# Layer 0's own part turned on VectorE and loaded from DRAM, two-direction operand products, fixed operand slots

## The chip, the cores and the metric

The kernel runs on one core of a Trainium2 chip. A core has a matrix engine (TensorE; PE in the profile, PEld for its weight loads), VectorE (DVE), ScalarE (ACT), GpSimd (POOL) and SyncE (SP), which here only issues DMAs. Sixteen DMA engines move data between DRAM and the on-chip memory SBUF. Matmul results go to PSUM, which has eight banks. Each engine works through its own instruction queue in order and waits on semaphores for the others.

The metric is the device time of one execution in microseconds. The time of the kernel before is a median of 2452.59 us over 3 runs (2452.18 to 2453.55).

## The reference

Two graph layers over 128 graphs of 64 nodes with 768 features, all in float32. The change touches only layer 0:

```python
h = jnp.maximum(_layernorm(x, axis=-1), 0.0)
ctx = jnp.matmul(adj, hs @ Wadj.T + badj) / deg_c[..., None]
ctx = ctx + jnp.matmul(radj, hs @ Wrev.T + brev) / rdeg_c[..., None]
ctx = ctx + hs @ Wself.T + bself
...
x = x + ctx + rel
```

Here `hs` is `h`, `adj` is the 0/1 (and id) matrix of a graph, `radj` its transpose, and `rel` a relation term that is computed through small tables of counts. So every node's new value has three parts that go through a 768x768 weight matrix: its neighbours along the edges, its neighbours against them, and itself. Layer 1 is graph attention with six heads, an exponential linear unit and a sigmoid gate. It is left as it is.

## The kernel before

Two graphs make a tile of 128 rows; the 64 tiles are worked in 32 pairs. For a tile, layer 0 needs the transposes of (adjacency / degree) x h for the two directions, and the transpose of h for the self part, as stationary operands of matmuls. `operands` (L582) makes them on TensorE: it multiplies a block of h (64 rows of one graph, 128 features) by `rts`, which holds for each graph two scaled adjacency matrices and an identity, side by side, 192 columns. So one product gives all three parts, turned, in PSUM, and a ScalarE copy (L599) brings 768 columns of them to SBUF. One call makes the operand `a{k}{q}` of tile k of the pair and a third q of the features; there are six calls per pair.

`main` (L609) multiplies the operands by the weights. It doesn't take all 18 block products but 15: `form` (L602) makes sums of operands (A_SUMS: f1 to f11) on VectorE, sums of weight blocks are made once, and 15 products of six matmuls each (L638) go to four PSUM banks, a to d. When a bank holds a partial sum that belongs to the output, VectorE adds it into x (`add`, L630 and L632), and the bank is then used further. Ninety such matmul steps make a pair's main loop. Pair 0 uses the plain 18 products.

`beside` (L780) lists what is done beside the main loop of pair p, each entry with the step before which it is emitted: for pair p-1 the end (`finish`: layer norm of the result for layer 1, output store, stores of two forms of it), for pair p+1 the preparation (adjacency, degrees, layer norm and relu, operands, sums of operands, counts). `merged` (L233) sorts the entries by step, entries of one step in the order of the list. All five queues, SP's too, are then executed in exactly this order: nothing is reordered in layer 0.

The order around the change, in the loop of pair p, is: step 0 the sums f5, f6, f3 of pair p; 20 degrees and relus of pair p+1; 30 `prep_c`; 32 layer-norm statistics of the first finished tile; 37 and 43 counts; 40 `norm_and_store` of it (VectorE's scaled mean L292, ScalarE's relu L671, GpSimd's addition L672, then SP's output store L673 and the store L676 of hh); 44 `turn_and_store` (VectorE's 32x32 block transpose L682 and SP's store L683); 46 two calls of `operands`; 49 statistics of the second tile; 53 sum f1; 55 and 59 its `norm_and_store` and `turn_and_store`; 58 two calls; 66 sums f7, f4 and the loads of pair p+2's adjacency and x; 70 two calls; 77 sums f8, f9, f2. Operands lie in a rotating set of 17 buffers named `op` and two named `oq`.

```python
(46, lambda: operands(n, 1, 2)),
(46, lambda: operands(n, 1, 1)),
(53, lambda: form(n, "f1")),
...
(58, lambda: operands(n, 0, 0)),
(58, lambda: operands(n, 0, 2)),
...
(70, lambda: operands(n, 1, 0)),
(70, lambda: operands(n, 0, 1)),
```

For layer 1 the kernel already has a way to turn a tile without TensorE: `turn_and_store` transposes 32x32 blocks on VectorE and stores them to DRAM, and `load_h` (L326) loads them back in pieces of 32 floats, which puts the blocks in their places. `load_h(0)` is emitted at step 30 of the last pair's loop, among the loads of layer 1's weights (`fetch`, L337).

## Time and profile before

| What | us |
|---|---|
| median of 3 runs | 2452.59 |
| the profiled execution's own time | 2452.42 |
| its span, first to last instruction | 2450.6 |
| TensorE busy | 2424.8 (99%) |
| VectorE busy | 2047.8 (84%) |
| ScalarE busy | 1025.6 (42%) |
| the main products of layer 0 in bank a (L638 pwa) | 547.7 |
| the products that make operands (L591) | 152.0 |
| the copies of operands (L599) | 121.1 |

The span is the time between the first and the last instruction of the profiled execution. Busy time is the union of an engine's instructions; a matmul record's end is modelled, and records overlap. A float32 matmul is two records. In the lists of instructions a line gives the code line, the engine, the operation, output and inputs by name, shapes, the count, and after the bar busy time, mean length of one in ns and the idle time of the engine before them with what ended most of it. In lines of waits the numbers are total us, times and the longest one.

### The profile page before, as it was taken

What the parts mean: (1) busy time and instruction counts of PE and PEld (TensorE: products, weight loads), DVE (VectorE), ACT (ScalarE), POOL (GpSimd) and SP (SyncE); (2) the same over time, 40 slices, a digit from 0 to 9 for tenths busy, and PEclk for the clock granted to TensorE, in tenths of its full rate; (3) what the DMA queues carried; (4) which work ended last, traced back from release to release, by engine and by line L of the source; (5) the groups of instructions that cost most, each with busy time, mean ns of one, the idle gap of its engine ahead of it and who ended that gap; (6) DMA issues with size and microseconds to landing.
All of it is one profiled execution on the core that took longest, in us unless ns stands there. A gap on an engine that the chain in (4) does not pass through costs nothing.

```text
span 2450.6 us, 34880 instructions
## 1 busy us (share of the span) xinstructions
PE 2424.8 (99%) x11777; PEld 1689.8 (69%) x11777; DVE 2047.8 (84%) x4169; ACT 1025.6 (42%) x3399; POOL 449.2 (18%) x799
## 2 busy tenths in 40 slices
PE   9999999999999999999999998999999999999997
PEld 7888888888888888888888885444444444444445
DVE  8888788788788788788788767789999989888999
ACT  2122222222222222122122122776777777777677
POOL 1112112112112112112122112111111111111122
PEclk9999999999999999999999999999999999999999
DMA  5112212212213113113113146565555555555544
GB/s 181 55 54 90 73 54 92 70 55 95 67 54 99 64 54 102 60 54 108 55 55 108 54 115 161 91 119 116 113 109 113 113 108 115 108 107 118 109 98 101
DMA packets 348660, 224.54 MB, mean 92 GB/s; under 512 B 236234, under 2 KB 298813, under 8 KB 348482
## 3 DMA queue, kind: packets, MB, share of 16 engines
q1 hardware_dynamic: 338610, 197.51, 30.0%
q0 software_dynamic: 9728, 24.78, 6.4%
q8 instruction: 92, 1.51, 0.2%
q14 instruction: 86, 0.70, 0.1%
q10 hardware_dynamic: 144, 0.04, 0.0%
HBM read 96.07 MB, written 100.66 MB: 80 GB/s over the span
## 4 chain that ended last, share of the span: by engine, by line
PE 93%; DVE 4%; ACT 1%; DMA 1%; issue 0%; SPq 0%; DVEq 0%; POOL 0%; ACTq 0%; POOLq 0%
PE pwa L638 20%; PE pwb L638 16%; PE pma L908 13%; PE pmb L908 11%; PE pwc L638 7%; PE pwd L638 7%; PE pb L591 6%; PE pmc L908 4%; PE pmd L908 4%; PE ps L1061 2%; PE pwd L622 1%; PE ps L1043 1%; DVE weights L309 1%; ACT pr L960 1%; PE ps L1012 0%
## 5 line engine op out<-in xcount | busy, mean ns | idle before, releaser
L638 PE MATMUL pwa<-weights,op 128*128 128x256 f32 x2304 | 547.7, 382 | 4.1 <-DVE x L630 2.6
L638 PEld LDWEIGHTS pwa<-weights,op 128*128 128x128 f32 x2304 | 420.8, 190 | 66.9 <-issue 7.6
L638 PE MATMUL pwb<-weights,op 128*128 128x256 f32 x1536 | 360.8, 381 | 0.3 <-DVE x L630 0.3
L638 PEld LDWEIGHTS pwb<-weights,op 128*128 128x128 f32 x1536 | 286.6, 190 | 44.4 <-issue 6.7
L908 PE MATMUL pma<-weights,op_f 128*128 128x512 f32 x620 | 310.3, 597 | 1.1 <-DVE weights L935 0.8
L288 POOL TENSOR_TENSOR rn<-ve,mhalf 128x1 f32<-128x1 f32 x128 | 93.5, 730 | 935.4 <-DVE ve L287 935.3
L309 DVE TENSOR_TENSOR op<-op 128x768 f32<-128x768 f32 x248 | 241.4, 993 | 1.2
L960 ACT ACTIVATE pr<-pr 128x128 f32<-128x128 f32 x768 | 225.3, 295 | 25.1 <-DVE pr L950 24.1
L488 ACT ACTIVATE h<-x,rn 128x768 f32<-128x768 f32 x64 | 62.4, 1020 | 383.1 <-DVE rn L292 364.2
L671 ACT ACTIVATE hf<-x,rn 128x768 f32<-128x768 f32 x64 | 65.7, 1027 | 357.6 <-DVE rn L292 349.3
L908 PEld LDWEIGHTS pma<-weights,op_f 128*128 128x128 f32 x620 | 112.2, 190 | 138.7 <-issue 103.2
L599 ACT COPY op<-pb 128x768 f32<-128x768 f32 x160 | 121.1, 797 | 180.0 <-PE pb L591 179.8
L908 PE MATMUL pmb<-weights,op_f 128*128 128x512 f32 x372 | 193.1, 601 | 0.4 <-DVE hz L935 0.4
L638 PE MATMUL pwc<-weights,op 128*128 128x256 f32 x780 | 187.0, 383 | 0.0
L638 PE MATMUL pwd<-weights,op 128*128 128x256 f32 x768 | 176.3, 379 | 0.0
L638 PEld LDWEIGHTS pwc<-weights,op 128*128 128x128 f32 x780 | 145.6, 190 | 25.2 <-issue 6.7
L672 POOL TENSOR_TENSOR x<-x,hf 128x768 f32<-128x768 f32 x64 | 135.7, 2121 | 133.4 <-ACT hf L671 133.4
L638 PEld LDWEIGHTS pwd<-weights,op 128*128 128x128 f32 x768 | 145.8, 190 | 20.0 <-issue 0.2
L591 PE MATMUL pb<-r,h 64*128 64x192 f32 x1536 | 152.0, 337 | 0.4 <-ACT h L488 0.4
L591 PEld LDWEIGHTS pb<-r,h 64*128 64x128 f32 x1536 | 123.0, 187 | 33.9 <-issue 23.0
L960 ACT ACTIVATION_READ_ACCUMULATOR pr<-pr 128x1 f32 x768 | 144.3, 188 | 0.0
L1033 ACT ACTIVATE pb<-al,mx 128x64 f32<-128x64 f32 x384 | 128.5, 337 | 12.4 <-DVE mx L1025 11.6
(210 smaller groups left out, 4143.6 us busy)
## 6 DMA issues: line engine op xcount, KB each, us to landing
x<-in_x_dram SPq DMA_DIRECT2D x64, 384.0 KB
out_dram<-x SPq DMA_DIRECT2D x64, 384.0 KB
hh<-hh SPq DMA_DIRECT2D x64, 384.0 KB
h<-ht SPq DMA_DIRECT2D x64, 384.0 KB
h<-h SPq DMA_DIRECT2D x256, 96.0 KB
x<-hh SPq DMA_DIRECT2D x64, 384.0 KB
out_dram<-f POOLq DMA_DIRECT2D x62, 384.0 KB, 4.7
hx<-weights SPq DMA_DIRECT2D x88, 192.0 KB
```

What stands on the lines that cost most here:

```text
L288: nc.gpsimd.tensor_tensor(to[:, 0:1], ve, mhalf, op=OP.pow)
L309: return (nc.vector.tensor_add if s1 == "+" else nc.vector.tensor_sub)(to, x, y)
L488: nc.scalar.activation(h, X[t], AF.Relu, scale=to[:, 0:1], bias=to[:, 1:2])
L591: nc.tensor.matmul(ps[:, g, i * 3 * N : (i + 1) * 3 * N], H0[t][s, kb * P : (kb + 1) * P], rts[p % 2][s, k].rearrange("p s n -> p (s n)"), ...
L599: nc.scalar.copy(a.rearrange("p h s (g n) -> p g (h s) n", g=GT), ps[:, :, : 6 * N].rearrange("p g (x n) -> p g x n", n=N))
L638: nc.tensor.matmul(bank[b][:, :CQ], OPS[p, an][:, q, s, :], bw[bn][:, (s * KQ + q) * CQ : (s * KQ + q + 1) * CQ], start=(first and q == s ...
L671: nc.scalar.activation(h, X[t], AF.Relu, scale=to[:, 0:1], bias=to[:, 1:2])
L672: nc.gpsimd.tensor_add(X[t], X[t], h)
L908: nc.tensor.matmul(bank[p, b], operand(p, an)[:, q, :], bw2[bn][:, 2 * q * CQ : 2 * (q + 1) * CQ], start=(first and q == 0), stop=(q == KQ ...
L960: nc.scalar.activation(PR[t][:, j, h, :], PR[t][:, j, h, :], AF.Copy, accum_out=to)
L1033: nc.scalar.activation(PB[t][:, h, :], AL[t][:, h, :], AF.Exp, bias=MX[t][:, h : h + 1], accum_out=DN[t][:, h : h + 1])
L1061: nc.tensor.matmul(po[r][o, c, :], PT[t][s, c, o], (hs if r == g else HX[t])[s, 2 * c + r, :], start=True, stop=True)
```

## The change

The self part no longer goes through TensorE for pairs 2 to 31. ScalarE computes the relu of a tile a second time (`relu_mixed`) with the columns of each 128-feature block permuted. VectorE transposes the 32x32 blocks of that (`turn_own`, steps 27 and 33), SP stores the result to a DRAM tile (H0D), and `load_own` (steps 40, 44 and 60, two operands at a time) loads it as the third part of the operand's buffer, in pieces of 32 floats. `operands` now takes two calls in one PSUM tile and multiplies by two directions only, 128 columns; the calls are one batch at step 70 and two at step 46, none at 58. The buffers of operands become named slots (`SLOTS`), each with its own tag, two of them double, and f3 and f2 are formed in place of a12 and a10. The order of the dimensions in an operand changes (part before half). Pairs 0 and 1 keep the products of three directions. `load_h(0)` moves from step 30 to step 62 of the last pair's loop.

```diff
 PLAIN = tuple((f"a{k}{j}", f"b{j}{q}", "abcdab"[2 * i + k], j == 0, f"{k}{q}" if j == 2 else None,
                "+", i > 0) for i, q in enumerate((0, 2, 1)) for k in range(2) for j in range(3))
+SLOTS = {"a12": "s0", "f3": "s0", "a00": "s1", "a02": "s2", "a01": "s3", "f1": "s4", "f7": "s5",
+         "f11": "s5", "f4": "s6", "f8": "s7", "f9": "s8", "f5": "s9", "f6": "s10", "f10": "s11",
+         "a11": "t0", "a10": "t1", "f2": "t1"}
+SLOTS0 = {"a00": "s7", "a01": "s9", "a02": "s10", "a12": "s11"}
+IN_PLACE = {"f3": "a12", "f2": "a10"}
 PLACES = ("g6", "g10", "b11", "b21", "g12", "w", "g14", "b01", "b10", "b20", "b02", "b12", "b22",
...
     NQ = P // Q
+    H0D = [dram.tile([KB * P, P], F32, name=f"h0_{t}") for t in range(NT)]
     H1D = [[dram.tile([KB * P, P], F32, name=f"h1_{p}_{k}") for k in range(2)] for p in range(NP)]
     def row(v, parts):
...
                     to[:, :, s, :],
                     src.rearrange("(j k p) n -> j p k n", k=KQ, p=P)[j][:, :, q * CQ : (q + 1) * CQ])
-        return ([(30, lambda: load_h(0)), (67, lambda: nc.sync.dma_start(hbb, row(hb, P)))]
+        return ([(62, lambda: load_h(0)), (67, lambda: nc.sync.dma_start(hbb, row(hb, P)))]
                 + [(i, lambda n=n: load_block(n)) for i, n in (
                     (7, "b10"), (13, "b00"), (13, "b21"), (25, "b11"), (31, "b01"), (37, "b20"),
                     (49, "b22"), (49, "b02"), (61, "b12"))]
...
             h = H0[t] = work.tile([P, D], F32, name="h0")
             nc.scalar.activation(h, X[t], AF.Relu, scale=to[:, 0:1], bias=to[:, 1:2])
+        HP = {}
+        def relu_mixed(t, to):
+            hp = HP[t] = work.tile([P, D], F32, name="hp", bufs=1)
+            nc.scalar.activation(
+                hp.rearrange("p (b f i) -> p b f i", b=KB, f=NQ),
+                X[t].rearrange("p (b i f) -> p b f i", b=KB, f=NQ),
+                AF.Relu, scale=to[:, 0:1], bias=to[:, 1:2])
+        def turn_own(t):
+            h = work.tile([P, D], F32, name="hpt", bufs=1)
+            nc.vector.transpose(h, HP[t])
+            nc.sync.dma_start(H0D[t].rearrange("(b p) n -> p b n", p=P),
+                              h.rearrange("p (b n) -> p b n", b=KB))
+        def new_operand(p, n):
+            tag = SLOTS0.get(n, SLOTS[n]) if p == 0 else SLOTS[n]
+            OPS[p, n] = work.tile([P, 3, KQ, P], F32, name="op", tag=tag,
+                                  bufs=2 if tag[0] == "t" else 1)
+            return OPS[p, n]
+        def load_own(p, *names):
+            for n in names:
+                k, q = int(n[1]), int(n[2])
+                nc.sync.dma_start(
+                    new_operand(p, n)[:, 2].rearrange("p b (a n) -> p (b a) n", a=NQ),
+                    H0D[2 * p + k].rearrange("(b i) (f n) -> (i f) b n", i=Q, n=Q)[
+                        :, q * KQ * NQ : (q + 1) * KQ * NQ, :])
         def prep(p):
             af = ADF[p] = work.tile([P, 2, 2, N], F32, name="af", bufs=1)
...
             for i, (a, b) in enumerate(PARTS):
                 nc.scalar.copy(cn[: 3 * (b - a), i, :], pn[: 3 * (b - a), i, :])
-        def operands(p, k, q):
-            t = 2 * p + k
+        def operands(p, *calls):
+            n = 2 if p in SHARED else 3
             ps = pss.tile([P, GT, 512], F32, name="pb")
-            for i in range(2):
-                kb = 2 * q + i
-                for g in range(GT):
-                    s = slice(g * N, (g + 1) * N)
-                    nc.tensor.matmul(ps[:, g, i * 3 * N : (i + 1) * 3 * N],
-                                     H0[t][s, kb * P : (kb + 1) * P],
-                                     rts[p % 2][s, k].rearrange("p s n -> p (s n)"),
-                                     start=True, stop=True)
-            a = OPS[p, f"a{k}{q}"] = (
-                work.tile([P, KQ, 3, P], F32, name="oq") if (k, q) == (1, 1) else
-                work.tile([P, KQ, 3, P], F32, name="op", bufs=17))
-            nc.scalar.copy(a.rearrange("p h s (g n) -> p g (h s) n", g=GT),
-                           ps[:, :, : 6 * N].rearrange("p g (x n) -> p g x n", n=N))
+            for c, (k, q) in enumerate(calls):
+                to = ps[:, :, c * n * KQ * N : (c + 1) * n * KQ * N].rearrange(
+                    "p g (s i n) -> p g s i n", s=n, i=KQ)
+                for i in range(KQ):
+                    kb = KQ * q + i
+                    for g in range(GT):
+                        o = slice(g * N, (g + 1) * N)
+                        nc.tensor.matmul(to[:, g, :, i, :],
+                                         H0[2 * p + k][o, kb * P : (kb + 1) * P],
+                                         rts[p % 2][o, k, :n].rearrange("p s n -> p (s n)"),
+                                         start=True, stop=True)
+            for c, (k, q) in enumerate(calls):
+                a = OPS[p, f"a{k}{q}"] if p in SHARED else new_operand(p, f"a{k}{q}")
+                nc.scalar.copy(
+                    a[:, :n].rearrange("p s h (g n) -> p g (s h) n", g=GT),
+                    ps[:, :, c * n * KQ * N : (c + 1) * n * KQ * N].rearrange(
+                        "p g (x n) -> p g x n", n=N))
+        SHARED = range(2, NP)
         def form(p, *names):
             for n in names:
                 s0, x, s1, y = A_SUMS[n]
-                t = OPS[p, n] = work.tile([P, KQ, 3, P], F32, name="op", bufs=17)
-                signed(t, s0, OPS[p, x], s1, OPS[p, y])
+                if n in IN_PLACE:
+                    OPS[p, n] = OPS[p, IN_PLACE[n]]
+                else:
+                    new_operand(p, n)
+                signed(OPS[p, n], s0, OPS[p, x], s1, OPS[p, y])
         def main(p):
...
                     if first and q == s == 0:
                         new(b)
                     nc.tensor.matmul(
-                        bank[b][:, :CQ], OPS[p, an][:, q, s, :],
+                        bank[b][:, :CQ], OPS[p, an][:, s, q, :],
                         bw[bn][:, (s * KQ + q) * CQ : (s * KQ + q + 1) * CQ],
                         start=(first and q == s == 0), stop=(q == KQ - 1 and s == 2),
                         skip_group_check=True)
...
             DEV[p] = deviations((2 * p, 2 * p + 1))
         def relus(p):
+            to, mv = DEV[p]
             for k in range(2):
-                mean_and_relu(2 * p + k, DEV[p][0][k], DEV[p][1][k])
+                t = 2 * p + k
+                if p in SHARED:
+                    scaled_mean(to[k], mv[k])
+                    relu_mixed(t, to[k])
+                    relu(t, to[k])
+                else:
+                    mean_and_relu(t, to[k], mv[k])
         def degrees_and_norms(p):
             rd = degrees(p)
...
-            (54, lambda: operands(1, 1, 2)),
-            (54, lambda: operands(1, 1, 1)),
+            (54, lambda: operands(1, (1, 2))),
+            (54, lambda: operands(1, (1, 1))),
...
                 (30, lambda: prep_c(n)),
                 (37, lambda: ids_worth(n, 0)),
                 (43, lambda: ids_sum(n, 0)),
-                (46, lambda: operands(n, 1, 2)),
-                (46, lambda: operands(n, 1, 1)),
+                (27, lambda: turn_own(2 * n)),
+                (33, lambda: turn_own(2 * n + 1)),
+                (40, lambda: load_own(n, "a12", "a11")),
+                (44, lambda: load_own(n, "a00", "a02")),
+                (60, lambda: load_own(n, "a10", "a01")),
+                (46, lambda: operands(n, (1, 2), (1, 1))),
+                (46, lambda: operands(n, (0, 0), (0, 2))),
                 (53, lambda: form(n, "f1")),
                 (56, lambda: ids_worth(n, 1)),
-                (58, lambda: operands(n, 0, 0)),
-                (58, lambda: operands(n, 0, 2)),
                 (61, lambda: ids_sum(n, 1)),
                 (64, lambda: digits(n)),
                 (66, lambda: form(n, "f7", "f4")),
                 (66, lambda: load(n + 1)),
-                (70, lambda: operands(n, 1, 0)),
-                (70, lambda: operands(n, 0, 1)),
+                (70, lambda: operands(n, (1, 0), (0, 1))),
                 (77, lambda: form(n, "f8", "f9", "f2")),
                 (80, lambda: count_t(n, 0)),
                 (85, lambda: count_t(n, 1))]
```

More of the change, by code (lines that the diff above doesn't have):

```diff
@@ L718 @@
         table_product(0)
-        operands(0, 0, 0)
+        operands(0, (0, 0))
         table_product(1)
@@ L722 @@
         table_copy()
-        operands(0, 0, 1)
+        operands(0, (0, 1))
         prep_c(0)
@@ L748 @@
             (2, lambda: ids_sum(0, 0)),
-            (4, lambda: operands(0, 0, 2)),
+            (4, lambda: operands(0, (0, 2))),
             (8, lambda: count(0, 1)),
-            (12, lambda: operands(0, 1, 0)),
-            (12, lambda: operands(0, 1, 1)),
-            (17, lambda: operands(0, 1, 2)),
+            (12, lambda: operands(0, (1, 0))),
+            (12, lambda: operands(0, (1, 1))),
+            (17, lambda: operands(0, (1, 2))),
             (18, lambda: table_part(0)),
@@ L774 @@
             (60, lambda: weights_sums("g12", "g5")),
-            (64, lambda: operands(1, 0, 0)),
-            (64, lambda: operands(1, 0, 2)),
+            (64, lambda: operands(1, (0, 0))),
+            (64, lambda: operands(1, (0, 2))),
             (66, lambda: weights_sums("g8")),
@@ L779 @@
             (76, lambda: weights_sums("g11", "g3")),
-            (80, lambda: operands(1, 1, 0)),
-            (80, lambda: operands(1, 0, 1)),
+            (80, lambda: operands(1, (1, 0))),
+            (80, lambda: operands(1, (0, 1))),
             (84, lambda: count_t(1, 0)),
```

## The prediction, made before the result was known

> **What bounds the kernel now.** I read the page first: the busy shares, the forty slices, the costly groups.

> ```profile
> span 2450.6 us, 34880 instructions
> ...
> PE 2424.8 (99%) x11777; PEld 1689.8 (69%) x11777; DVE 2047.8 (84%) x4169; ACT 1025.6 (42%) x3399; POOL 449.2 (18%) x799
> ...
> L591 PE MATMUL pb<-r,h 64*128 64x192 f32 x1536 | 152.0, 337 | 0.4 <-ACT h L488 0.4
> L591 PEld LDWEIGHTS pb<-r,h 64*128 64x128 f32 x1536 | 123.0, 187 | 33.9 <-issue 23.0
> L599 ACT COPY op<-pb 128x768 f32<-128x768 f32 x160 | 121.1, 797 | 180.0 <-PE pb L591 179.8
> ```

> TensorE is busy for 99% of the span and its groups wait for almost nothing: layer 0 is a stream of matmuls. The operand batches start 45.7 us apart in every pair of tiles (780.9, 826.6, 872.3 us), so I studied one pair, 806.28 to 852.01 us, by windows, and then who waited for whom in layer 0.

> ```profile
> 806.28:852.01 45.73, 45.73 (x247) 38.79 (x246) 36.74 (x75) 11.01 (x16) 8.51 (x8) 1.00 0.22 72
> ...
> DVE x L630 <- PE pwa L622: 76.7, 30, 2.6
> DVE x L630 <- PE pwb L622: 61.6, 30, 2.1
> DVE x L630 <- PE pwc L622: 44.9, 30, 1.6
> ```

> The first line gives busy time of PE, PEld, DVE, ACT and POOL, the granted clock (1.00) and the DMA share. VectorE works 36.74 of 45.73 us. Its free 9 us are mostly three waits for TensorE near the end of a pair: 76.7/30 = 2.6, 2.1 and 1.5 us. Before them VectorE lags, and its order matters. The timeline shows that stretch (start, length, engine, line):

> ```profile
> 826.14 0.15 DVE L292 SCALAR_TENSOR_TENSOR rn<-mv,rn 128x1 f32<-128x1 f32 x1
> 826.39 1.03 ACT L671 ACTIVATE hf<-x,rn 128x768 f32<-128x768 f32 x1 [7.98 <-DVE rn L292]
> 826.59 1.57 PE L591 MATMUL pb<-r,h 64*128 64x192 f32 x16
> 827.49 1.82 POOL L672 TENSOR_TENSOR x<-x,hf 128x768 f32<-128x768 f32 x1 [2.90 <-ACT hf L671]
> 829.34 0.34 SPq L673 DMA_DIRECT2D out_dram<-x  x1
> 829.73 0.44 SPq L676 DMA_DIRECT2D hh<-hh  x1
> 830.57 0.37 SPq L683 DMA_DIRECT2D h<-ht  x1
> 830.96 0.95 DVE L309 TENSOR_TENSOR op<-oq,op 128x768 f32<-128x768 f32 x1
> 832.41 0.15 DVE L292 SCALAR_TENSOR_TENSOR rn<-mv,rn 128x1 f32<-128x1 f32 x1
> 836.26 0.34 SPq L673 DMA_DIRECT2D out_dram<-x  x1
> 843.81 0.95 DVE L309 TENSOR_TENSOR op<-op 128x768 f32<-128x768 f32 x1
> 846.53 0.41 DVE L632 TENSOR_TENSOR x<-x,pwa 128x256 f32<-128x256 f32 x1
> 848.84 0.59 PE L638 MATMUL pwa<-weights,op 128*128 128x256 f32 x2
> ```

> The reader should see two things. From the scaled mean (step 40, 826.14) to the output store's issue (829.34) lie 3.2 us through ScalarE and GpSimd, and SP, which issues in program order, stands still until then; VectorE reaches the sum f1 (step 53) only 4.82 us after that mean. And the read of bank a after product f5 (846.53) stands behind f8, f9 and f2 (from 843.81); product f2 reuses that bank at 848.84, 1.9 us after the read ends.

> **What the change removes from TensorE.** A two-call batch is 16 records, two rows of 64 side by side, so eight steps; the records start 0.1625 us apart (322 ns each, overlapping). It holds the stream for 1.70 us: the next product starts at 829.06 instead of 824.77 + 2.59 = 827.36. So 1.30 us are steps and 0.40 us turning in and out. With 128 instead of 192 columns a step scales to 0.108 us, which is also the distance of two weight loads in the present batch, so both fit. One visit with two batches plus one with one: 2 x 0.40 + 24 x 0.108 = 3.40 us instead of 5.10: 1.70 us less per pair. Thirty pairs (2 to 31) are built this way, beside main loops 1 to 30: at most 51 us. If the weight load bounded the step at the present 0.1625, only the dropped visit, 0.40 us, would remain.
> [...]

> **What it removes and adds elsewhere.** The copies shrink from 768 to 512 columns (797 ns, 0.53 by columns), six per pair: ScalarE gains 1.6 us and loses two more relus (L488, 1.02 us each); it is busy 11 of 45.7 us, so this is free unless the permuted read more than doubles the relu. The relu of the second tile waits for the first transpose to free its buffer; it then ends about 821, the plain relu behind it, on which the operands wait, about 822 (needed at 826.6), and the second transpose comes at 823.9. VectorE gains two transposes of 0.97 us (the row of L682). The first lands in a wait for TensorE of 0.8 us at step 29, so the scaled mean of step 40 moves from 826.14 to about 827.2. The transposed store needs about 3 us alone, issued near 820.3; the second transpose overwrites its buffer at 823.9: free, or 1 us if a transfer is late. The in-place sums and fixed slots remove no instruction: each slot's last reader is steps ahead of its next writer.

> SP gets eight more DMAs: two stores, six loads of 1024 pieces of 128 bytes. SP waits at steps 27 and 33 for VectorE with nothing behind it before the output store of step 40, and both stores have landed by about 828, before any load asks for them. Layer 1's loads of such pieces are the row: 1536 took 1.43 us of packets, so 2048 take 1.9 us. DMA share rises from 22% to some 40%, no bound. The second batch of operands, at step 70, stays where it was; the loads of x, 3.6 us later on SP, still have 10 us before their use.

> **Where the new wait is.** The loads of a12 and a11 stand at step 40, behind the output and hh stores of that step. With the mean at 827.2 the output store goes at 830.4. The semaphore increments of the trace put its landing 2.34 us after its issue and hh's 1.1 us later; the loads' packets follow: landing about 830.4 + 3.4 + 1.9 = 835.8. VectorE reaches f1 at 830.96 + 1.1 = 832.05 and waits 3.75 us. Behind f1 stand the read of bank d, the scaled mean of step 55, the counts, a transpose and every later read. That mean moves to 837.15, its output store (836.26 - 832.41 = 3.85 later) to 841.0; hh and ht land at +3.4 and +4.85 (trace), and a10 0.95 later: 846.8. VectorE gets to f8 about 846.1, so f8 starts at 846.85, the read after f5 ends 3.15 later (846.94 - 843.81), at 850.0, with 0.1 for the restart f2's product starts at 850.1 instead of 848.84. TensorE alone would be there at 848.84 - 1.7 = 847.1. So it stands for 3.0 us, and the pair takes 45.73 + 1.3 = 47.0 us. VectorE then again waits for the product f2, so each pair starts alike: 30 x 1.3 = +39 us.

> The bounds of a load's landing: alone, layer 1's single load of 768 pieces ends 2.1 us after issue; unqueued, f1 would get its data 2 us earlier, VectorE would be ready for f8 at 844.1, the read would end at 847.25, and TensorE would hardly wait. Queued behind one late ring (an output store landed after 4.1 instead of 2.3 us once), each of the two critical landings is 1.7 us later: 3 us more per pair, were it every pair. I take the FIFO value: the adjacency load, queued the same way behind ht, lands 0.25 us after ht.
> [...]

> **The last pair.** load_h(0) moves from step 30 to 62. Now its eight DMAs (4.86 us on SP) stand ahead of weight loads for which VectorE waits 4.3, 2.9 and 2.0 us, and TensorE then stands 3.9 us. Moved, it may give back up to 4 us, or cost 2 at the start of layer 1: I take -3. Sum against the profiled execution: 2452.4 (span 2450.6 and 1.8 around it, 0.2 under the median) + 39 - 3 = 2488.

> **The rivals.** A, the forecast: loads behind stores, 2488; its own range 2468 to 2512 (0.7 us per pair either way). B, the data lands early enough that VectorE's idle end swallows the wait: the read after f5 must end 2.9 us earlier than in A, of which f8's own wait gives 0.75, so the wait at f1 must stay under 3.75 - 2.15 = 1.6 us. Then pairs take 44.0: a gain of 51 + 3, or less where part of the wait shows: 2398 to 2440. For it: 6 us of waiting at the pair's end; against: SP's order and the 4.82 us between mean and f1. C, the copies, which write two thirds of the tile that the DMA writes into, wait for that DMA: the copies of a00 and a02 then hold ScalarE until 839.5, the second output store goes 2.2 us later and the pair takes 49.2: 2452 + 104 - 3 = 2553. For it: one tile, two writers; against: the two halves of the adjacency are issued one behind the other with no wait for landing. D, TensorE does not get faster (0.40 us instead of 1.70) while VectorE decides anyway: the same 2488, so it changes only B, to 2437. E, gain and wait cancel, 2448 to 2457: both landings 0.65 us earlier than in A do it.

> **How the numbers follow.** A 0.54, B 0.26, C 0.12, E 0.04, D 0 of its own; 0.04 for mishaps beyond. Within 0.2% (about what can be told from no change here) is 2447.7 to 2457.5. Faster is B: 0.26. Slower is A, C and most of the rest: 0.70. The range runs from the middle of B's gain, 2408, to short of C, 2532.

> **What would show it.** Right: matmuls of 64x128 some 0.108 us apart; VectorE waiting 3 to 4 us in every pair before the L309 sum f1, ended by a DMA; TensorE waiting about 3 us per pair on pwa for VectorE's read. Wrong: no DMA among VectorE's waits (B), or ScalarE's copies waiting for a DMA (C).

## The result, and the profile after

The changed kernel takes 2540.21 us (median of 4 runs, 2520.61 to 2544.22) against 2453.07 us: a ratio of 1.034, 95% interval 1.0286 to 1.0393. The forecast had the direction, 2488 us, with an upper bound of 2532 us that the result lies beyond (one of the four executions, 2520.61, lies inside it). The four differ by 24 us, those of before by under 2 us, and the granted TensorE clock goes with it: 0.988 of full speed in the fastest, 0.978 in the slowest, a difference of about 0.010 x 2530 = 25 us. The profiled execution took 2539.87 us, 87.5 us more than that of before. The page first: the span, the busy times and the costliest groups.

```profile
span 2537.6 us, 35543 instructions
...
PE 2420.1 (95%) x11777; PEld 1686.7 (66%) x11777; DVE 2088.9 (82%) x4229; ACT 1088.1 (43%) x3459; POOL 430.6 (17%) x799
...
L690 PE MATMUL pwa<-weights,op 128*128 128x256 f32 x2304 | 578.8, 400 | 94.1 <-DVE x L684 90.7
...
L319 DVE TENSOR_TENSOR op<-op 128x768 f32<-128x768 f32 x310 | 298.3, 986 | 153.4 <-DMA op<-h 151.1
L506 ACT ACTIVATE hp<-x,rn 128x768 f32<-128x768 f32 x60 | 107.2, 1786 | 427.4 <-DVE rn L302 400.8
```

TensorE falls from 99% to 95% of the span. Two waits that were not there carry it: VectorE waits 151 us for DMAs at the sums of operands (L319), TensorE 91 us for VectorE's reads of bank a (L684). The permuted relu (L506) takes 1.79 us, not the 1.02 of the plain one. Who waited for whom in layer 0 (total, times, longest):

```profile
DVE op L319 <- DMA op<-h: 151.1, 59, 5.2
DVE x L682 <- PE pwa L674: 126.7, 30, 6.0
PE pwa L690 <- DVE x L684: 87.4, 30, 7.0
```

Two DMA waits in nearly every one of 30 pairs, and one stand of TensorE (time in which it waits idle) in each. The timeline of one pair shows them in their order, the lines answering to those of before:

```profile
829.73 2.06 PE L638 MATMUL pb<-r,h 64*128 64x128 f32 x32
830.16 0.15 DVE L302 SCALAR_TENSOR_TENSOR rn<-mv,rn 128x1 f32<-128x1 f32 x1
831.45 1.82 POOL L724 TENSOR_TENSOR x<-x,hf 128x768 f32<-128x768 f32 x1 [3.72 <-ACT hf L723]
833.30 0.35 SPq L725 DMA_DIRECT2D out_dram<-x  x1
833.74 0.38 SPq L728 DMA_DIRECT2D hh<-hh  x1
834.23 1.66 SPq L529 DMA_DIRECT2D op<-h  x2
838.61 0.96 DVE L319 TENSOR_TENSOR op<-op 128x768 f32<-128x768 f32 x1 [3.62 <-DMA op<-h]
839.82 0.15 DVE L302 SCALAR_TENSOR_TENSOR rn<-mv,rn 128x1 f32<-128x1 f32 x1
843.66 0.35 SPq L725 DMA_DIRECT2D out_dram<-x  x1
849.68 2.82 DVE L319 TENSOR_TENSOR op<-op 128x768 f32<-128x768 f32 x3 [1.07 <-DMA op<-h]
852.42 0.41 DVE L684 TENSOR_TENSOR x<-x,pwa 128x256 f32<-128x256 f32 x1
852.89 1.22 PE L690 MATMUL pwa<-weights,op 128*128 128x256 f32 x2 [2.37 <-DVE x L684]
854.11 2.34 PE L690 MATMUL pwa<-weights,op 128*128 128x256 f32 x5
```

SP stands at the output store until 833.30, the loads of a12 and a11 go out at 834.23, and VectorE waits 3.62 us for them at f1. Those of a10 and a01 go out at 845.06, behind the next tile's stores, and VectorE waits 1.07 us at f8. The read after f5 comes at 852.42, and TensorE has then stood for 2.37 us. The last line holds what the forecast did not: five records take 2.34 us, where twelve took 2.75. The granted clock, by windows, just after that stand and just after that (PE, PEld, DVE, ACT and POOL busy, then the clock):

```profile
852.90:856.20 3.30, 3.30 (x9) 2.65 (x10) 0.27 (x1) 0.43 (x2) 0.00 (x0) 0.50 0.03 11
856.30:859.70 3.40, 3.40 (x19) 2.93 (x18) 1.88 (x4) 0.00 (x0) 0.00 (x0) 1.00 0.00 0
```

After the stand TensorE runs 3.4 us at half its clock. Between 100 us and the last operand batch the trace has 20 such stretches, 81.9 us in all; before the change there is none in that part. One came later there, in the last pair: after a stand of 2.33 us twelve records take 4.54 us, and the next twelve 2.75.

```profile
1481.47 4.54 PE L638 MATMUL pwa<-weights,op 128*128 128x256 f32 x12 [2.33 <-DVE x L630]
1485.85 2.75 PE L638 MATMUL pwb<-weights,oq 128*128 128x256 f32 x12
```

The sum of the 87.5 us, by pairs: eight of the 29 distances between operand batches are 46.7 to 47.4 us, thirteen 48.3 to 48.6, which is 46.7 and the 1.7 us that one half-clock stretch costs, and eight 48.9 to 54.4, against 45.73 before. An undisturbed pair, 46.7, is 30 x 0.97 = 29 us. Stands that late transfers made longer than the usual 2.35 us add 87.4 - 30 x 2.35 = 17 us. The longest, 7.0 us, comes once and not from an operand: in the loop of pair 3 VectorE waits 5.7 us for the load of layer 1's attention bias (`bb`), which stands behind the new loads on SP; before the change it waited 0.9 us there. Half of 81.9 us at half clock adds 41. Together 87.

### The profile page after: what moved, and what is told of

The parts are those of the page before. It is cut to its first block, busy times and chain, and to the rows that moved or that the text cites. A ratio compares the mean times of both kernels' runs of the same rounds, so it can differ in the third digit from the quotient of the medians.

```text
span 2537.6 us, 35543 instructions
## 1 busy us (share of the span) xinstructions
PE 2420.1 (95%) x11777; PEld 1686.7 (66%) x11777; DVE 2088.9 (82%) x4229; ACT 1088.1 (43%) x3459; POOL 430.6 (17%) x799
## 4 chain that ended last, share of the span: by engine, by line
PE 57%; DVE 22%; DMA 12%; issue 3%; ACT 3%; POOL 2%; SPq 2%; DVEq 0%; ACTq 0%; POOLq 0%
PE pma L969 12%; PE pwa L690 11%; PE pmb L969 10%; DMA op<-h 10%; PE pwb L690 6%; DVE op L319 5%; PE pmc L969 4%; PE pmd L969 4%; PE pwd L690 3%; DVE sum L593 2%; DVE eq L585 2%; POOL x L724 2%; PE ps L1122 2%; DVE eq L588 1%; ACT hf L723 1%
## 5 line engine op out<-in xcount | busy, mean ns | idle before, releaser
L690 PE MATMUL pwa<-weights,op 128*128 128x256 f32 x2304 | 578.8, 400 | 94.1 <-DVE x L684 90.7
L690 PEld LDWEIGHTS pwa<-weights,op 128*128 128x128 f32 x2304 | 445.8, 201 | 167.5 <-DVE x L684 99.5
L690 PE MATMUL pwb<-weights,op 128*128 128x256 f32 x1932 | 456.4, 382 | 0.8 <-DVE x L684 0.4
L319 DVE TENSOR_TENSOR op<-op 128x768 f32<-128x768 f32 x310 | 298.3, 986 | 153.4 <-DMA op<-h 151.1
L690 PEld LDWEIGHTS pwb<-weights,op 128*128 128x128 f32 x1932 | 359.2, 190 | 51.7 <-DVE x L684 1.9
L506 ACT ACTIVATE hp<-x,rn 128x768 f32<-128x768 f32 x60 | 107.2, 1786 | 427.4 <-DVE rn L302 400.8
L298 POOL TENSOR_TENSOR rn<-ve,mhalf 128x1 f32<-128x1 f32 x128 | 73.7, 576 | 916.1 <-DVE ve L297 916.0
L682 DVE TENSOR_TENSOR x<-pwa,x 128x256 f32<-128x256 f32 x95 | 39.1, 411 | 138.7 <-PE pwa L674 130.1
L624 ACT COPY cntT<-pb 126x128 bf16<-126x128 bf16 (+1 forms) x128 | 27.6, 269 | 286.2 <-PE pb L621 286.2
L294 DVE BATCH_NORM_STATS2 st<-x 128x6 f32<-128x384 f32 x256 | 129.0, 545 | 2.6 <-DMA x<-in_x_dram 2.5
```

The lines of the kernel that those rows point to most:

```text
L294: nc.vector.bn_stats(st[:, i, :], src[:, i * HALF : (i + 1) * HALF])
L298: nc.gpsimd.tensor_tensor(to[:, 0:1], ve, mhalf, op=OP.pow)
L319: return (nc.vector.tensor_add if s1 == "+" else nc.vector.tensor_sub)(to, x, y)
L506: nc.scalar.activation(hp.rearrange("p (b f i) -> p b f i", b=KB, f=NQ), X[t].rearrange("p (b i f) -> p b f i", b=KB, f=NQ), AF.Relu, scal ...
L690: nc.tensor.matmul(bank[b][:, :CQ], OPS[p, an][:, s, q, :], bw[bn][:, (s * KQ + q) * CQ : (s * KQ + q + 1) * CQ], start=(first and q == s ...
```

## The experiments

The theory after the result: the loads of the turned tiles stand behind stores in SP's order; VectorE waits for them; behind its sums stands the read that TensorE needs; and TensorE's clock is halved when it has stood. The rivals: the added work of turning (ScalarE's second relu, VectorE's transposes, the DMA traffic) is too much wherever the loads stand; the halved clock comes from something else; the small pieces, not the place in the queue, make the wait. Every ratio is to the kernel before.

**Both loads ahead of the stores.** Only the steps of two entries move.

```diff
-                (40, lambda: load_own(n, "a12", "a11")),
+                (39, lambda: load_own(n, "a12", "a11")),
...
-                (60, lambda: load_own(n, "a10", "a01")),
+                (54, lambda: load_own(n, "a10", "a01")),
```

> The loads of a12, a11 are issued at step 39 and those of a10, a01 at step 54, ahead of the output and hh stores of steps 40 and 55; nothing else changes. Theory (VectorE waits for loads that stand behind the stores on SP): no DMA among VectorE's waits at the sums, TensorE doesn't stand at bank a, no half-clock stretches, 44.0 to 44.3 us per pair, 2398 to 2410 us in all. Rival (the added transposes, relus and DMA traffic of turning make the pair longer wherever the loads stand): 2480 us or more.

Measured: 2409.87 us, 0.9825 (0.981 to 0.984). Its waits in layer 0 up to 1520 us:

```profile
DVE x L682 <- PE pwa L674: 81.0, 31, 3.4
DVE x L682 <- PE pwb L674: 56.0, 28, 2.1
...
DVE op L319 <- DMA op<-h: 0.7, 2, 0.5
...
PE pwa L690 <- DVE x L684: 6.1, 3, 3.3
```

Of VectorE's waits for a DMA at the operand sums 0.7 us are left, two times, where there were 151 us; VectorE waits for TensorE again, as before the change. All pairs but two (45.4 and 46.1) are 44.12 us apart, and there is no half-clock stretch between 100 us and the last operand batch. The order of two entries on SP is worth 130 us, and with it the change is a gain of 1.75%. SP's part of the timeline, with VectorE's f1, shows why:

```profile
803.74 0.15 DVE L302 SCALAR_TENSOR_TENSOR rn<-mv,rn 128x1 f32<-128x1 f32 x1
...
804.35 1.62 SPq L529 DMA_DIRECT2D op<-h  x2
...
806.87 0.35 SPq L725 DMA_DIRECT2D out_dram<-x  x1
807.32 0.38 SPq L728 DMA_DIRECT2D hh<-hh  x1
...
808.52 0.96 DVE L319 TENSOR_TENSOR op<-op 128x768 f32<-128x768 f32 x1
```

The loads go out 2.5 us ahead of the output store, in time in which SP only waited, and f1 starts without a wait 4.8 us after the mean, as it did before the change. By the semaphore increments the second load lands 3.6 us after the first one's issue here, and 4.3 us after it in the pair shown of the changed kernel: counted from its issue it lands 0.7 us later behind the stores, and the rest of what the new place gives is SP's wait for the output store's data.

**Dummy matmuls where TensorE stands.**

```diff
+                (84, lambda: keep_awake(22)),
```

> The changed kernel with 22 dummy bf16 matmuls (0.107 us each by the row of the same matmuls at the start of the kernel, 2.35 us) ahead of product f2, where TensorE stands 2.4 to 3 us. Theory (the halved clock is an answer to TensorE standing): the 20 or so half-clock stretches of 3.4 us in layer 0, 82 us in all, go away, and half of that, 41 us: 2493 to 2505 us. Rival (the halved clock has another source, the batches of small matmuls or the load of the chip): the stretches stay, 2535 us or more.

Measured: 2508.07 us, 1.0233 (1.0215 to 1.025), 32 us less than the changed kernel, for 22 matmuls whose results nobody reads.

```profile
DVE op L319 <- DMA op<-h: 148.3, 59, 4.6
...
PE pwa L690 <- DVE x L684: 48.1, 30, 5.2
```

VectorE's waits are those of the changed kernel. The stands are shorter, mostly 1.1 us and not gone: the dummies start 0.056 us apart here, not 0.107 as at the start of the kernel, so 22 of them fill 1.2 us. Of the half-clock stretches 17 us are left, where late transfers made a stand longer. So the halved clock answers to the stand. Most pairs are 46.8 us apart, the undisturbed pair of the changed kernel. The 17 us that are left cost half of that, 8.5 us: 2540.2 - 41 + 8.5 = 2508, which is where the time lies, 3 us above the expected range.

**Turning alone.** No loads, and the operand products make all three parts again.

```diff
-            n = 2 if p in SHARED else 3
+            n = 3
...
-                (40, lambda: load_own(n, "a12", "a11")),
-                (44, lambda: load_own(n, "a00", "a02")),
-                (60, lambda: load_own(n, "a10", "a01")),
-                (46, lambda: operands(n, (1, 2), (1, 1))),
-                (46, lambda: operands(n, (0, 0), (0, 2))),
+                (46, lambda: operands(n, (1, 2))),
+                (46, lambda: operands(n, (1, 1))),
...
+                (58, lambda: operands(n, (0, 0))),
+                (58, lambda: operands(n, (0, 2))),
```

> The turning stays (second relu, transposes on VectorE, stores to DRAM), the loads of the turned tiles are left out, and the operand products make all three parts again, one call at a time at steps 46, 58 and 70. Theory: TensorE bounds every pair as before, 45.7 us, and the added work lies in VectorE's 9 free us: 2448 to 2458 us. Rival (the added work on VectorE and ScalarE itself makes the pair longer): 2480 us or more.

Measured: 2452.02 us, 0.9998 (0.9988 to 1.0007); all pairs but one (46.1) 45.7 us apart. Two transposes, two relus of 1.79 us and two stores per pair cost nothing: VectorE's free time and ScalarE's hold them. The rival of too much work on VectorE and ScalarE falls; that the loads' traffic isn't too much either is what the kernel with both loads first shows.

**Only a10 and a01 first.**

```diff
-                (60, lambda: load_own(n, "a10", "a01")),
+                (54, lambda: load_own(n, "a10", "a01")),
```

> Only the loads of a10 and a01 move ahead of the second tile's stores (step 54); a12 and a11 stay behind the first tile's. Theory: VectorE's wait of 3.6 us at f1 stays, that of 1.1 us at f8 goes, TensorE stands 1.1 us less per pair, about 1.3 us by the records, which is too short to halve the clock: 45.7 us per pair, 2445 to 2460 us. If the clock is halved as often as before: about 2490. If the wait at f8 is what counts alone: about 2400.

Measured: 2467.67 us, 1.0056 (1.0039 to 1.0073).

```profile
DVE op L319 <- DMA op<-h: 114.0, 30, 5.2
...
PE pwa L690 <- DVE x L684: 49.5, 31, 5.0
```

The 30 waits that are left are those at f1, 114.0/30 = 3.8 us; those at f8 are gone. Twenty-two of the pairs are 45.5 to 45.9 us apart, as expected; seven pairs with late transfers, 46.3 to 51 us, and 17 us at half clock up to the last operand batch put the time 8 us above the expected range. One us less of wait per pair is worth 72 us, since the clock then mostly stays up.

**Only a12 and a11 first.**

```diff
-                (40, lambda: load_own(n, "a12", "a11")),
+                (39, lambda: load_own(n, "a12", "a11")),
```

> Only the loads of a12 and a11 move ahead of the first tile's stores (step 39); a10 and a01 stay at step 60 behind the second tile's. Theory: the wait at f1 goes, the mean of step 55 and all behind it come 3.6 us earlier, a10 too, so VectorE's idle end covers what is left at f8: 44.1 to 44.5 us per pair, 2407 to 2420 us, as with both pairs of loads moved. Rival (each of the two waits costs what it measured): 1.1 us per pair stays, 2440 to 2450 us.

Measured: 2414.99 us, 0.9849 (0.9836 to 0.9862).

```profile
DVE op L319 <- DMA op<-h: 28.6, 28, 2.3
...
PE pwa L690 <- DVE x L684: 10.7, 4, 3.9
```

A wait at f8 is left in 26 of the pairs, mostly 0.85 us, and yet nearly all pairs are 44.1 us apart and TensorE stands only 4 times: VectorE's idle end hides it. Two waits on one engine are not worth what each measures: in most pairs the second costs nothing once the first is gone. Of the 9.6 us between the profiled executions of this kernel and of the one with both loads first, 8.7 lie in two early pairs (50.0 and 50.3 us against 45.4 and 46.1).

**Larger pieces in the same place.**

```diff
-                    new_operand(p, n)[:, 2].rearrange("p b (a n) -> p (b a) n", a=NQ),
-                    H0D[2 * p + k].rearrange("(b i) (f n) -> (i f) b n", i=Q, n=Q)[
-                        :, q * KQ * NQ : (q + 1) * KQ * NQ, :])
+                    new_operand(p, n)[:, 2],
+                    H0D[2 * p + k].rearrange("(b p) n -> p b n", p=P)[
+                        :, q * KQ : (q + 1) * KQ, :])
```

> Every load stays in its place behind the stores, but reads the turned tile in pieces of 512 bytes (256 of them instead of 1024 of 128 bytes); the 32x32 blocks are then not put in their places, so the self part of the operands is left unassembled. Theory (the place in the queue is most of the wait): by the packets of the trace before (27.7 ns each instead of 13.7) a load takes 0.44 us instead of 0.88, so f1 waits 2.7 us instead of 3.6 and f8 0.6 instead of 1.1, the pair takes about 45.5 us with the clock seldom halved: 2440 to 2465 us. Rival (the small pieces are the cause): the wait at f1 falls under 1.5 us, 2400 to 2420 us.

Measured: 2476.69 us, 1.0101 (1.0088 to 1.0115).

```profile
DVE op L319 <- DMA op<-h: 110.7, 56, 5.2
...
PE pwa L690 <- DVE x L684: 50.3, 30, 5.5
```

The waits shrink by a quarter, from 151 to 111 us: at f1 from mostly 3.6 to 3.0 us (2.7 expected, under 1.5 by the rival), at f8 from 1.1 to 0.6. Most pairs come to 45.6 us. The pieces are part of the cost, the place in the queue is most of it. The time is 12 us above the expected range, for the same reason as in the kernel with a10 first: eight pairs with late transfers take 46.2 to 52 us, and 24 us up to the last operand batch pass at half clock.

**load_h(0) back to step 30**, on the kernel with both loads first.

```diff
-        return ([(62, lambda: load_h(0)), (67, lambda: nc.sync.dma_start(hbb, row(hb, P)))]
+        return ([(30, lambda: load_h(0)), (67, lambda: nc.sync.dma_start(hbb, row(hb, P)))]
```

> The kernel with both pairs of loads ahead of the stores, and load_h(0) back at step 30 of the last pair's loop. The prediction took 3 us for its move to step 62. By the trace of the kernel with the loads first, the last pair takes about 1 us longer than before the change, so theory now: the move only changes which weights VectorE waits for: 2405 to 2413 us, no difference to 2409.9. If the prediction's term was right: about 2413.

Measured: 2408.25 us (2407.38 to 2412.05), 0.9821 (0.9807 to 0.9834), against 2409.87 with step 62: no difference that can be told from noise, and the kernel without the move isn't the slower one. The 3 us of the forecast don't show.

**Two weight sums later in the last pair**, on the kernel with both loads first.

```diff
-                    (22, "g10"), (28, "g6"), (41, "g12"), (46, "u"), (50, "g14"), (57, "w"),
-                    (59, "g5"), (65, "v"), (67, "g3"), (70, "g9"), (73, "g1"), (76, "g8"),
+                    (22, "g10"), (28, "g6"), (41, "g12"), (46, "u"), (50, "g14"), (66, "w"),
+                    (68, "g5"), (65, "v"), (67, "g3"), (70, "g9"), (73, "g1"), (76, "g8"),
```

> The kernel with both pairs of loads ahead of the stores, and in the last pair's loop the weight sums w and g5 moved from steps 57 and 59 to 66 and 68, since VectorE waits 5.2 us for their blocks there with the reads of the banks behind it, and TensorE then stands 1.6 and 3.3 us and runs 3.4 us at half clock. Theory: 3 to 5 us less, 2405 to 2407 us. If the wait only moves on to later sums: 2410, no difference.

Measured: 2407.54 us (2406.36 to 2408.09), 0.9817 (0.9804 to 0.9831), half a us above the expected range and the lowest of all, though its interval overlaps that of the kernel it was built on. One of the two stands in the last pair went, the other grew from 3.3 to 4.0 us. That it is better than the kernel with both loads first is likely, not shown.

## Why the prediction was wrong

- **TensorE's gain** was 1.70 us per pair in the forecast and 45.73 - 44.12 = 1.61 us in the kernel where nothing else stands in the way. The steps of an operand batch are 0.112 us apart where 0.108 was expected; the weight loads, 0.188 us by their records and two to a step, are hidden in steps of that length. In the trace the batch's matmul records start in pairs, 0.007 us apart, and the record of the next weight load starts 0.002 to 0.003 us after each of them, while the matmul's record goes on for 0.272 us; by what means they overlap no run here shows.
- **The hidden work** was hidden: turning alone measured 0.9998. The permuted relu at 1.79 us was 1.75 times the plain one and still free, as the forecast allowed up to twice.
- **The wait at f1** was forecast at 3.75 us and is 3.62 in the pair shown, 3.6 in most pairs and 3.8 on average. In most pairs the semaphore increments put a11's landing 5.1 to 5.2 us after the output store's issue, forecast 5.3 (830.4 + 3.4 + 1.9 is 835.7, from which its 837.15 follows, and not 835.8; the wait is then 3.65). Packets of 128 bytes took 13.0 ns on average in the changed kernel's layer 0, against 13.7 in layer 1 of the kernel before. The wait at f8 was forecast at 0.75 and is mostly 1.1.
- **The stand** was forecast at 3.0 us and is mostly 2.3 to 2.5 by the records, 46.7 - 44.1 = 2.6 by the pairs; the undisturbed pair, forecast at 47.0, is 46.7. Up to here rival A described the mechanism, and its direction was no luck.
- **What failed** is the step "the pair takes 45.73 + 1.3 = 47.0 us. VectorE then again waits for the product f2, so each pair starts alike: 30 x 1.3 = +39 us". It let TensorE go on at full clock after standing and every pair start alike; thirteen pairs are 48.3 to 48.6 us long. The trace before had a hint in the last pair: a stand of 2.33 us, and the clock at half for 3.4 us from 0.9 us after it. The term for the halved clock was left out; it measured 41 us in the profiled run.
- **A second term was missing there**: transfers that come late now stand on the path. The forecast named one late ring as a bound and gave its mean no weight; it is 17 us, 4.7 of them from the one wait for `bb`, which the forecast didn't look at; what makes the others late isn't shown.
- **The last pair's 3 us** don't show: in the kernel with the loads first, with the load of h moved away, VectorE waits 5.2 and 2.1 us for later blocks (4.3, 2.9 and 2.0 before), and TensorE stands 1.6 and 3.3 us in that pair (2.3 and 1.5 before).

The range was set by the landing of the loads alone, with 2532 at its top; clock and late transfers together lay outside it. Rival C, ScalarE's copies waiting for the DMA, didn't occur: no DMA ended a wait of the copies. Rival B is what the kernel with the loads first shows: 44.1 us per pair.

## What to carry to other kernels

SP issues in program order here, and a load that was put behind a store inherited that store's wait for its data (behind it the first load went out 0.9 us after the store's issue, ahead of it 2.5 us before) and landed 0.7 us later after its own issue. When an entry is added to such a list, ask what stands ahead of it at that step: here moving two entries, one by a step and one by six, turned 3.4% slower into 1.75% faster. Where a new wait makes TensorE stand for more than some two microseconds at a time, ask for the granted clock after it: here each stretch of 3.4 us at half clock added 1.7 us to the sum.

## What the runs showed of the hardware

The relu whose input is read every fourth float, 16 bytes apart, took 1.786 us against 1.020 for the same columns in order. No run here shows what the difference comes from.
